# Taking whole-tile elementwise work off GpSimd in a statically scheduled four-layer graph network

## Chip, cores, metric

One NeuronCore of a Trainium2 chip. The metric is the device time of one execution in microseconds (us). Ratios are the mean time of one kernel's runs over the mean of the other kernel's runs of the same rounds, so they differ a little from the ratio of the medians that are quoted.

## What is computed

In this kernel TensorE (PE in the views) does the matrix products and leaves them in PSUM, a memory of banks; ScalarE (ACT) and VectorE (DVE) read them out, which is called an eviction below, and work elementwise; GpSimd (POOL) works elementwise too. GAT is a graph attention layer.

64 graphs of 256 nodes with 256 features pass four layers, each with a residual and a norm:

```python
x = _layernorm(x + L0(x, adj))   # 8-head masked attention, norm, feed-forward (256 -> 1024 -> 256), norm
x = _layernorm(x + L1(x, adj))   # GAT: softmax_m(leaky(f_n + g_m) masked) @ (x W^T) + bias
x = _layernorm(x + L2(x, adj))   # GAT, then elu
x = _layernorm(x + L3(x, adj))   # two relational graph convolutions with elu
```

L1 adds `attn1[:, :, None] + attn2[:, None, :]`, applies leaky_relu (slope 0.2), masks, and takes a softmax. All products are float32.

## The kernel before

The kernel doesn't issue instructions as it meets them. It records operations of all graphs (engine, assumed cost, tiles read and written), lets a list scheduler choose one static order, and then issues them in that order; every engine works through its own part of it in sequence.

```python
class Plan:
    LAG = {"PE": 0.21, "DVE": 0.13, "ACT": 0.13, "POOL": 0.08, "SP": 3.5}
    SWITCH = 0.3                       # assumed cost of a change of matmul shape on TensorE
    # op(): dependencies by tile, or by part of a tile: (t, part)
    # schedule(): earliest operation of the oldest graph that can start, engine by engine [cut]
...
        for o in plan.schedule():
            o.issue()
```

`port="uses"` marks operations of VectorE and GpSimd that the plan never lets overlap across these two engines. PSUM is held by a ring of four one-bank tiles ("bank") and a single four-bank tile ("wide"), which QKV, the scores and the feed-forward use in turn:

```python
                    act(1.02, ... nc.scalar.activation(ph(), s()[:, :, hg, :], AF.Exp, accum_out=...), [s], [ph])
                    # masks of p: first half on VectorE, second half on GpSimd
                    op("DVE" if hg == 0 else "POOL", 1.14 if hg == 0 else 2.1, mask, [ph, am], [ph], port="uses")
...
            def feed_forward(x1, xt):
                add_row(xt, ln2b)                                     # GpSimd
                ...                                                   # x1 *= ln1g, x1 += b2: GpSimd
                hid, w = new("hid", [P, NF, N]), new("wide", None)
                def chunk(f):
                    return w()[:, f % 4, f // 4, :]                   # bank f % 4
                for f in range(NF):                                   # 8 chunks
                    pe("full", 0.86, ... product(chunk(f), w1.., x1T..), [x1T], [(w, f % 4)], [hid])
                    act(0.36, ... activation(hid()[:, f, :], chunk(f), AF.Relu, bias=..), [(w, f % 4)], [(hid, f)])
                y = product_plus(... w2 ..., x1)
                mv, rstd = statistics(y, False)
                # apply: four fused VectorE steps: (y - mean) * ln2g, then * rstd + xt
                dve(2.4, apply, [y, mv, rstd, xt], [y], "uses")
                layer_norm(y)
```

A norm is bn_stats and bn_aggr on VectorE, four operations on 128x2 elements on GpSimd (rstd and the shift), and the application on ScalarE. The GAT's score chain:

```python
                for i in range(NB):
                    act(0.36, ... activation(e()[:, i, :], pf(), AF.Identity, bias=g_i), [pf, (h, i)], [(e, i)])
                dve(0.60, ... e = max(0.2 * e, e))
                act(0.52, ... e = exp(e))
                dve(0.60, ... e = min(e, gm))                         # gm is 1e30 on an edge, else 1e-30
```

## Time and profile before

| | before |
|---|---|
| time, median | 3626.88 us (3623.37 to 3631.0, 4 runs) |
| TensorE busy | 3220.8 us, 89% |
| VectorE, ScalarE, GpSimd busy | 2294.5, 1587.1, 1591.0 us |
| mean granted TensorE clock | 0.959 |
| TensorE waits, all rows of its view summed | 397.8 us |

In the profile, lines such as `PE wide L561 <- ACT hid L707` name who waited (TensorE, for an instruction writing tile wide), for whom (ScalarE's instruction writing hid), then total us, times and longest. The reading is in the prediction below.

### The profile page before, as it was taken

How to read it: one execution, taken by the hardware profiler on the slowest of the kernel's cores; microseconds unless marked ns; L12 is line 12 of the kernel's file. 1: busy time of each engine (PE TensorE's matmuls, PEld its weight loads, DVE VectorE, ACT ScalarE, POOL GpSimd, SP SyncE). 2: the span in 40 equal slices, each digit the busy share in tenths (PEclk: the TensorE clock that was granted, in tenths of full speed). 3: DMA queues.
4: the chain of work that ended last, by engine and by line, in shares of the span. 5: the costliest groups of instructions: out<-in, count | busy, mean ns of one | idle time of the engine just before them, and what ended most of it. 6: DMA issues, size and time to landing. Idle time of an engine off the chain costs nothing.

```text
span 3632.6 us, 50464 instructions
## 1 busy us (share of the span) xinstructions
PE 3220.8 (89%) x18742; PEld 2357.1 (65%) x18742; DVE 2294.5 (63%) x4960; ACT 1587.1 (44%) x3393; POOL 1591.0 (44%) x2325
## 2 busy tenths in 40 slices
PE   5899998998988998989998989998998998998985
PEld 4666766666666766666766666766666766666663
DVE  3457656666666666666666666666666666666653
ACT  1334544444444444444444444444444444444442
POOL 3334444445444444444444444444444444354441
PEclk9999999999999999999999999999999999999997
DMA  4000000000010000010000000000000000000000
GB/s 121 12 15 30 30 24 21 27 24 30 18 30 21 30 21 24 23 30 21 27 24 21 27 30 21 27 24 21 27 30 21 27 24 21 27 30 24 12 4 10
DMA packets 91947, 93.64 MB, mean 26 GB/s; under 512 B 5648, under 2 KB 90896, under 8 KB 91696
## 3 DMA queue, kind: packets, MB, share of 16 engines
q1 hardware_dynamic: 87040, 83.91, 7.5%
q10 hardware_dynamic: 4032, 5.24, 0.4%
q8 instruction: 151, 2.47, 0.3%
q0 software_dynamic: 624, 1.19, 0.2%
q14 instruction: 100, 0.82, 0.1%
HBM read 73.54 MB, written 16.78 MB: 25 GB/s over the span
## 4 chain that ended last, share of the span: by engine, by line
PE 73%; DVE 11%; ACT 9%; POOL 3%; issue 2%; DMA 0%; SPq 0%; POOLq 0%; DVEq 0%; ACTq 0%
PE bank L561 42%; PE wide L561 20%; PE bank L673 5%; PE bank L552 4%; ACT hid L707 3%; ACT X L589 2%; PE wide L650 2%; DVE st L570 2%; DVE e L747 2%; ACT p L656 2%; DVE o L829 1%; DVE mv L571 1%; DVE X L689 1%; POOL rstd L577 1%; POOL rstd L575 1%
## 5 line engine op out<-in xcount | busy, mean ns | idle before, releaser
L561 PE MATMUL wide<-T,W1T 128*128 128x256 f32 x2048 | 535.2, 396 | 124.9 <-ACT hid L707 86.3
L561 PEld LDWEIGHTS wide<-T,W1T 128*128 128x128 f32 x2048 | 371.0, 192 | 264.3 <-ACT hid L707 153.6
L561 PE MATMUL bank<-cw,T 128*128 128x512 f32 x1024 | 471.3, 603 | 3.1 <-ACT T L555 3.0
L561 PE MATMUL bank<-W2T,hid 128*128 128x256 f32 x2048 | 465.5, 381 | 0.2 <-DVE X L773 0.2
L561 PEld LDWEIGHTS bank<-W2T,hid 128*128 128x128 f32 x2048 | 385.1, 190 | 53.0 <-issue 1.8
L574 POOL TENSOR_SCALAR rstd<-mv 128x2 f32<-128x2 f32 x384 | 104.7, 273 | 673.1 <-DVE mv L571 659.7
L589 ACT ACTIVATE X<-X,rstd 128x256 f32<-128x256 f32 x512 | 279.1, 595 | 261.8 <-POOL rstd L578 261.4
L707 ACT ACTIVATE hid<-wide,col_b 128x256 f32<-128x256 f32 x512 | 229.3, 471 | 292.8 <-PE wide L561 292.6
L561 PE MATMUL bank<-h,e 128*128 128x259 f32 x1024 | 304.8, 444 | 40.4 <-DVE e L747 40.1
L660 POOL TENSOR_TENSOR p<-p,am 128x1024 f32<-128x1024 f32 x128 | 278.0, 2172 | 138.8 <-ACT p L656 138.8
L561 PEld LDWEIGHTS bank<-cw,T 128*128 128x128 f32 x1024 | 193.4, 192 | 208.7 <-issue 188.6
L656 ACT ACTIVATE p<-wide 128x1024 f32<-128x1024 f32 x256 | 259.9, 1019 | 154.4 <-PE wide L650 154.4
L575 POOL TENSOR_TENSOR rstd<-rstd,neghalf 128x2 f32<-128x2 f32 x384 | 290.8, 757 | 32.0
L561 PEld LDWEIGHTS bank<-h,e 128*128 128x128 f32 x1024 | 218.2, 221 | 99.9 <-DVE e L747 59.6
L677 DVE RECIPROCAL inv<-bank 128x256 f32<-128x256 f32 x128 | 223.7, 1748 | 67.7 <-PE bank L673 67.6
L570 DVE BATCH_NORM_STATS2 st<-X 128x6 f32<-128x256 f32 x640 | 259.1, 405 | 8.7 <-POOL X L777 5.0
L561 PE MATMUL wide<-T,WqkvT 128*128 128x256 f32 x1024 | 251.0, 393 | 10.5 <-ACT p L656 9.3
L561 PE MATMUL bank<-gw,T 128*128 128x258 f32 x1024 | 249.9, 386 | 4.0 <-ACT T L555 2.6
L650 PE MATMUL wide<-qk 32*128 32x256 f32 x2048 | 162.6, 435 | 98.6 <-ACT p L656 93.4
L555 ACT COPY T<-bank 128x512 f32<-128x512 f32 x384 | 217.9, 589 | 65.9 <-PE bank L552 65.5
L845 POOL TENSOR_TENSOR o<-o,X 128x512 f32<-128x512 f32 x64 | 91.9, 1436 | 332.1 <-DVE o L829 332.1
L660 DVE TENSOR_TENSOR p<-p,am 128x1024 f32<-128x1024 f32 x128 | 186.5, 1457 | 65.5 <-ACT p L656 65.1
(126 smaller groups left out, 5801.0 us busy)
## 6 DMA issues: line engine op xcount, KB each, us to landing
adj<-in_adj_dram SPq DMA_DIRECT2D x128, 256.0 KB, 3.5
x<-in_x_dram SPq DMA_DIRECT2D x64, 256.0 KB, 2.7
xr<-in_x_dram SPq DMA_DIRECT2D x64, 256.0 KB, 2.7
out_dram<-o SPq DMA_DIRECT2D x64, 256.0 KB, 2.2
W1T<-in_W1T_dram ACTq DMA_DIRECT2D x1, 1024.0 KB, 9.5
W2T<-in_W2T_dram ACTq DMA_DIRECT2D x1, 1024.0 KB, 16.1
WqkvT<-in_WqkvT_dram ACTq DMA_DIRECT2D x1, 768.0 KB, 4.8
cw<-in_w_root_dram ACTq DMA_DIRECT2D x2, 256.0 KB, 12.6
```

What stands on the lines that cost most here:

```text
L552: nc.tensor.transpose(pt()[:, kb, i * P : (i + 1) * P], xt()[:, i, kb * P : (kb + 1) * P], ident)
L555: act(0.48, lambda: nc.scalar.copy(xT(), pt()), [pt], [xT])
L561: nc.tensor.matmul(dst, lhsT=lhs(c), rhs=rhs(c), start=(c == 0), stop=(c == n - 1))
L570: nc.vector.bn_stats(stat()[:, i, :], y()[:, i, :])
L575: nc.gpsimd.tensor_tensor(rstd()[:, 0, :], rstd()[:, 0, :], neghalf[:, 0:NB], op=ALU.pow)
L589: nc.scalar.activation(y()[:, i, :], y()[:, i, :], AF.Identity, bias=rstd()[:, 1, i : i + 1], scale=rstd()[:, 0, i : i + 1])
L650: nc.tensor.matmul(s()[:, r, hg, :], lhsT=qk()[f, KB + hg, kt * P : (kt + 1) * P], rhs=qk()[f, hg, :], start=True, stop=True)
L656: act(1.02, lambda ph=ph, k=k, s=s, hg=hg: nc.scalar.activation(ph(), s()[:, :, hg, :], AF.Exp, accum_out=seen_sum[:, k : k + 1]), [s], [ph])
L660: eng.tensor_tensor(ph(), ph(), am()[:, kt, None, :].to_broadcast([P, 4, N]), op=ALU.mult)
L673: nc.tensor.matmul(pc()[32 * r : 32 * r + 32, dst, :], lhsT=lhsT, rhs=p[kt, hg]()[:, r, :], start=(kt == 0), stop=(kt == NB - 1))
L677: dve(1.67, lambda hg=hg, pc=pc: nc.vector.reciprocal(inv()[:, hg, :], pc()[:, 1, :]), [pc], [(inv, hg)])
L707: act(0.36, lambda f=f: nc.scalar.activation(hid()[:, f, :], chunk(f), AF.Relu, bias=b1[:, f : f + 1]), [(w, f % 4)], [(hid, f)])
```

## The change

Its intent is to leave GpSimd little but the norms' 128x2 operations, so that its long whole-tile operations neither stand in chains nor block VectorE. The core of the diff (a constant tile for the bias, the checks at the end, repeated edits and a new sequence of the norms' bn_stats and bn_aggr are cut):

```diff
-            def add_row(xt, row):
-                pool(1.23, lambda: nc.gpsimd.tensor_tensor(xt(), xt(), row[...], op=ALU.add), [xt], [xt])
+            def with_row(xt, row, op):
+                dve(0.60, lambda: nc.vector.tensor_tensor(xt(), xt(), row[...], op=op), [xt], [xt], "uses")
+            def add(xt, yt):
+                dve(0.60, lambda: nc.vector.tensor_tensor(xt(), xt(), yt(), op=ALU.add), [xt, yt], [xt], "uses")
...
-                dve(0.33, ... tensor_scalar(gm(), pt(), BIG, TINY, op0=ALU.mult, op1=ALU.max), [pt], [gm])
+                dve(0.33, ... tensor_scalar(gm(), pt(), BIG, NO_EDGE, op0=ALU.mult, op1=ALU.add), [pt], [gm])   # -346
...
-                        op("DVE" if hg == 0 else "POOL", 1.14 if hg == 0 else 2.1, mask, [ph, am], [ph], port="uses")
+                        dve(1.14, mask, [ph, am], [ph], "uses")
...
-                pool(1.23, lambda: nc.gpsimd.tensor_tensor(seen_inv, seen_inv, inv(), op=ALU.add), [inv], [])
+                act(0.61, lambda: nc.scalar.activation(inv(), inv(), AF.Identity, accum_out=seen_inv[:, g : g + 1]), ...)
...   (feed-forward)
-                dve(2.4, apply, [y, mv, rstd, xt], [y], "uses")        # four fused steps
+                layer_norm(y)                                          # applied on ScalarE
+                with_row(y, ln2g, ALU.mult)
+                add(y, xt)
                 layer_norm(y)
...   (GAT)
-                    act(0.29, ... copy(h()[:, i, 0 : D + 2], ph()), [ph], [(h, i)])
+                    # layer 1: the bias is added in the eviction, on VectorE (0.34); layer 2 as before
...
-                    act(0.36, ... activation(e()[:, i, :], pf(), AF.Identity, bias=g_i), ...)
+                    dve(0.40, ... scalar_tensor_tensor(e()[:, i, :], pf(), g_i, gm()[:, i, :], op0=ALU.add, op1=ALU.min), ...)
...
-                dve(0.60, lambda: nc.vector.tensor_tensor(e(), e(), gm(), op=ALU.min), [e, gm], [e], "uses")
...   (layer 2: elu and residual in three fused VectorE steps; the last residual by add)
```

More of the change, by code (lines that the diff above doesn't have):

```diff
@@ L21 @@
 BIG = 1e30
-TINY = 1e-30
+NO_EDGE = -346.0
 RINGS = {"x": 3, "adj": 4, "bits": 2, "am": 2, "gm": 6, "T": 5, "qk": 2, "v": 2, "p": 6, "inv": 1, "ctxT": 2, "X": 9,
@@ L266, in weight, with rows @@
         return w
-    def rows(name):
+    def rows(name, zeros=0):
         v = t[name]
         n = v.shape[0]
-        w = const.tile([P, n], F32, tag=f"row_{name}", name=f"row_{name}")
-        nc.gpsimd.dma_start(w, bass.AP(tensor=v.tensor, offset=v.offset, ap=[[0, P], [1, n]]))
+        w = const.tile([P, n + zeros], F32, tag=f"row_{name}", name=f"row_{name}")
+        if zeros:
+            nc.vector.memset(w[:, n:], 0.0)
+        nc.gpsimd.dma_start(w[:, 0:n], bass.AP(tensor=v.tensor, offset=v.offset, ap=[[0, P], [1, n]]))
         return w
@@ L331, in tile_gnn_stack @@
     seen_sum = filled([P, 4 * B], F32, "seen_sum", 0.0)
-    seen_inv = filled([P, KB, N], F32, "seen_inv", 0.0)
+    seen_inv = filled([P, B], F32, "seen_inv", 0.0)
     seen_fg = filled([P, 2 * B, NB, 2], F32, "seen_fg", 0.0)
@@ L354, in tile_gnn_stack @@
     gat1 = gat_weights(1, "L1_WT", "L1_W")
-    gbias = rows("L1_bias")
+    gbias = rows("L1_bias", 2)
     gat2 = gat_weights(2, "L2_W", "L2_WT")
@@ L539, in load @@
                 return xt
-            def add_row(xt, row):
-                pool(1.23, lambda: nc.gpsimd.tensor_tensor(xt(), xt(), row[:, None, :].to_broadcast([P, NB, D]),
-                                                           op=ALU.add), [xt], [xt])
+            def with_row(xt, row, op):
+                dve(0.60, lambda: nc.vector.tensor_tensor(xt(), xt(), row[:, None, :].to_broadcast([P, NB, D]), op=op),
+                    [xt], [xt], "uses")
+            def add(xt, yt):
+                dve(0.60, lambda: nc.vector.tensor_tensor(xt(), xt(), yt(), op=ALU.add), [xt, yt], [xt], "uses")
             def transposed(xt):
@@ L561, in product, with layer_norm @@
                     nc.tensor.matmul(dst, lhsT=lhs(c), rhs=rhs(c), start=(c == 0), stop=(c == n - 1))
-            def statistics(y, shift):
+            def layer_norm(y):
                 mv, stat = new("mv", [P, NB, 2]), new("st", [P, NB, 6])
@@ L570, in stats @@
                         nc.vector.bn_stats(stat()[:, i, :], y()[:, i, :])
+                    for i in range(NB):
                         nc.vector.bn_aggr(mv()[:, i, :], stat()[:, i, :])
                 def root():
-                    nc.gpsimd.tensor_scalar(rstd()[:, 0, :], mv()[:, :, 1], EPS, None, op0=ALU.add)
+                    nc.gpsimd.tensor_scalar(rstd()[:, 0, :], mv()[:, :, 1], 1.0, EPS, op0=ALU.mult, op1=ALU.add)
                     nc.gpsimd.tensor_tensor(rstd()[:, 0, :], rstd()[:, 0, :], neghalf[:, 0:NB], op=ALU.pow)
-                    if shift:
-                        nc.gpsimd.tensor_tensor(rstd()[:, 1, :], mv()[:, :, 0], rstd()[:, 0, :], op=ALU.mult)
-                        nc.gpsimd.tensor_scalar(rstd()[:, 1, :], rstd()[:, 1, :], -1.0, None, op0=ALU.mult)
-                dve(1.08, stats, [y], [mv, stat])
-                pool(1.56 if shift else 1.0, root, [mv], [rstd], port="waits")
-                return mv, rstd
-            def layer_norm(y):
-                mv, rstd = statistics(y, True)
+                    nc.gpsimd.tensor_tensor(rstd()[:, 1, :], mv()[:, :, 0], rstd()[:, 0, :], op=ALU.mult)
+                    nc.gpsimd.tensor_scalar(rstd()[:, 1, :], rstd()[:, 1, :], -1.0, 1.0, op0=ALU.mult, op1=ALU.mult)
                 def apply():
@@ L590, in apply @@
                                              scale=rstd()[:, 0, i : i + 1])
+                dve(1.0, stats, [y], [mv, stat])
+                pool(1.5, root, [mv], [rstd], port="waits")
                 act(1.0, apply, [y, rstd], [y])
@@ L606, in masks @@
                 pe("full", 0.22, issue, [bits], [pt], [am, gm])
-                dve(0.33, lambda: nc.vector.tensor_scalar(gm(), pt(), BIG, TINY, op0=ALU.mult, op1=ALU.max), [pt], [gm])
+                dve(0.33, lambda: nc.vector.tensor_scalar(gm(), pt(), BIG, NO_EDGE, op0=ALU.mult, op1=ALU.add), [pt], [gm])
                 dve(0.33, lambda: nc.vector.tensor_tensor(am(), pt(), bits(), op=ALU.max), [pt, bits], [am])
@@ L657, in attention, with mask @@
                             ph(), s()[:, :, hg, :], AF.Exp, accum_out=seen_sum[:, k : k + 1]), [s], [ph])
-                        def mask(ph=ph, kt=kt, eng=nc.vector if hg == 0 else nc.gpsimd):
-                            eng.tensor_tensor(ph(), ph(), am()[:, kt, None, :].to_broadcast([P, 4, N]), op=ALU.mult)
-                        op("DVE" if hg == 0 else "POOL", 1.14 if hg == 0 else 2.1, mask, [ph, am], [ph], port="uses")
+                        def mask(ph=ph, kt=kt):
+                            nc.vector.tensor_tensor(ph(), ph(), am()[:, kt, None, :].to_broadcast([P, 4, N]), op=ALU.mult)
+                        dve(1.14, mask, [ph, am], [ph], "uses")
                 inv = new("inv", [P, KB, N])
@@ L679, in attention @@
                         ctxT()[:, hg, :], pc()[:, 0, :], inv()[:, hg, :], op=ALU.mult), [pc, (inv, hg)], [(ctxT, hg)])
-                pool(1.23, lambda: nc.gpsimd.tensor_tensor(seen_inv, seen_inv, inv(), op=ALU.add), [inv], [])
+                act(0.61, lambda: nc.scalar.activation(inv(), inv(), AF.Identity, accum_out=seen_inv[:, g : g + 1]), [inv], [inv])
                 return ctxT
@@ L692, in feed_forward @@
             def feed_forward(x1, xt):
-                add_row(xt, ln2b)
+                with_row(xt, ln2b, ALU.add)
                 x1T = transposed(x1)
-                pool(1.23, lambda: nc.gpsimd.tensor_tensor(x1(), x1(), ln1g[:, None, :].to_broadcast([P, NB, D]),
-                                                           op=ALU.mult), [x1], [x1])
-                add_row(x1, b2)
+                with_row(x1, ln1g, ALU.mult)
+                with_row(x1, b2, ALU.add)
                 hid, w = new("hid", [P, NF, N]), new("wide", None)
@@ L709, in feed_forward, with gat @@
                 y = product_plus(lambda c: hid()[:, c, :], [hid], lambda c: w2[:, c, :], NF, x1)
-                mv, rstd = statistics(y, False)
-                def apply():
-                    for i in range(NB):
-                        yi = y()[:, i, :]
-                        nc.vector.scalar_tensor_tensor(yi, yi, mv()[:, i, 0:1], ln2g, op0=ALU.subtract, op1=ALU.mult)
-                        nc.vector.scalar_tensor_tensor(yi, yi, rstd()[:, 0, i : i + 1], xt()[:, i, :],
-                                                       op0=ALU.mult, op1=ALU.add)
-                dve(2.4, apply, [y, mv, rstd, xt], [y], "uses")
+                layer_norm(y)
+                with_row(y, ln2g, ALU.mult)
+                add(y, xt)
                 layer_norm(y)
                 return y
-            def gat(xt, w, gm, seen, finish):
+            def gat(xt, w, gm, seen, bias, finish):
                 xT = transposed(xt)
@@ L729, in gat @@
                                                                 lambda kb: w[:, kb, :], KB), [xT], [ph], [h])
-                    act(0.29, lambda i=i, ph=ph: nc.scalar.copy(h()[:, i, 0 : D + 2], ph()), [ph], [(h, i)])
+                    if bias is None:
+                        act(0.29, lambda i=i, ph=ph: nc.scalar.copy(h()[:, i, 0 : D + 2], ph()), [ph], [(h, i)])
+                    else:
+                        dve(0.34, lambda i=i, ph=ph: nc.vector.tensor_tensor(h()[:, i, 0 : D + 2], ph(), bias, op=ALU.add),
+                            [ph], [(h, i)])
                 pool(0.1, lambda: (nc.gpsimd.memset(h()[:, :, ONE : ONE + 1], 1.0)), [], [(h, "one")], None)
@@ L742, in gat @@
                 for i in range(NB):
-                    act(0.36, lambda i=i: nc.scalar.activation(e()[:, i, :], pf(), AF.Identity,
-                                                               bias=h()[:, i, G_COL : G_COL + 1]), [pf, (h, i)], [(e, i)])
-                dve(0.60, lambda: nc.vector.scalar_tensor_tensor(e(), e(), SLOPE, e(), op0=ALU.mult, op1=ALU.max), [e], [e], "uses")
+                    dve(0.40, lambda i=i: nc.vector.scalar_tensor_tensor(e()[:, i, :], pf(), h()[:, i, G_COL : G_COL + 1],
+                                                                         gm()[:, i, :], op0=ALU.add, op1=ALU.min),
+                        [pf, (h, i), gm], [(e, i)])
+                dve(0.60, lambda: nc.vector.scalar_tensor_tensor(e(), e(), SLOPE, e(), op0=ALU.mult, op1=ALU.max), [e], [e],
+                    "uses")
                 act(0.52, lambda: nc.scalar.activation(e(), e(), AF.Exp), [e], [e])
-                dve(0.60, lambda: nc.vector.tensor_tensor(e(), e(), gm(), op=ALU.min), [e, gm], [e], "uses")
                 for i in range(NB):
@@ L757, in finish @@
                 def finish(i, z, po, r):
-                    if i == 0:
-                        add_row(xt, gbias)
                     dve(0.40, lambda: nc.vector.scalar_tensor_tensor(z()[:, i, :], po()[:, 0:D], r(), xt()[:, i, :],
                                                                      op0=ALU.mult, op1=ALU.add), [po, r, xt], [(z, i)])
-                z = gat(xt, gat1, gm, 2 * g, finish)
+                z = gat(xt, gat1, gm, 2 * g, gbias, finish)
                 layer_norm(z)
@@ L768, in finish @@
                 def finish(i, z, po, r):
-                    n = new("n", [P, D])
+                    n, zi = new("n", [P, D]), lambda: z()[:, i, :]
                     act(0.36, lambda: nc.scalar.activation(n(), po()[:, 0:D], AF.Exp, scale=r()), [po, r], [n])
-                    dve(0.30, lambda: nc.vector.tensor_scalar(n(), n(), 1.0, -1.0, op0=ALU.min, op1=ALU.add), [n], [n], "uses")
-                    dve(0.40, lambda: nc.vector.scalar_tensor_tensor(z()[:, i, :], po()[:, 0:D], r(), n(), op0=ALU.mult,
-                                                                     op1=ALU.max), [po, r, n], [(z, i)])
-                z = gat(xt, gat2, gm, 2 * g + 1, finish)
-                pool(1.23, lambda: nc.gpsimd.tensor_tensor(z(), z(), xt(), op=ALU.add), [z, xt], [z])
+                    dve(0.40, lambda: nc.vector.scalar_tensor_tensor(zi(), po()[:, 0:D], r(), xt()[:, i, :], op0=ALU.mult,
+                                                                     op1=ALU.add), [po, r, xt], [(z, i)])
+                    dve(0.37, lambda: nc.vector.scalar_tensor_tensor(n(), n(), 1.0, xt()[:, i, :], op0=ALU.min,
+                                                                     op1=ALU.add), [n, xt], [n], "uses")
+                    dve(0.37, lambda: nc.vector.scalar_tensor_tensor(zi(), n(), -1.0, zi(), op0=ALU.add, op1=ALU.max),
+                        [n, (z, i)], [(z, i)], "uses")
+                z = gat(xt, gat2, gm, 2 * g + 1, None, finish)
                 layer_norm(z)
@@ L835, in graph @@
             xT = transposed(xt)
-            add_row(xt, bo)
+            with_row(xt, bo, ALU.add)
             ctxT = attention(xT, am)
@@ L844, in graph @@
             h = conv(conv(xt, conv_w[0], conv_b[0], rel, rdeg), conv_w[1], conv_b[1], rel, rdeg)
-            pool(1.23, lambda: nc.gpsimd.tensor_tensor(h(), h(), xt(), op=ALU.add), [h, xt], [h])
+            add(h, xt)
             layer_norm(h)
@@ L860, in tile_gnn_stack @@
     nc.vector.tensor_reduce(worst[:, 0:1], seen_sum, AX.X, ALU.max)
-    nc.vector.tensor_reduce(worst[:, 1:2], seen_inv.rearrange("p h n -> p (h n)"), AX.X, ALU.add)
+    nc.vector.tensor_reduce(worst[:, 1:2], seen_inv, AX.X, ALU.max)
     nc.vector.tensor_reduce(worst[:, 2:3], seen_fg.rearrange("p g n k -> p (g n k)"), AX.X, ALU.max)
@@ L973, in general_layer1 @@
         z = general_gat("x3", xt, gat1, mask, ALU.add)
-        add_row(z, gbias)
+        add_row(z, gbias[:, 0:D])
         nc.gpsimd.tensor_tensor(z, z, xt, op=ALU.add)
```

## The prediction

> **What bounds the kernel now.** I read the page's busy shares first, then the slices, the waits of TensorE, and the timeline around the longest wait. In the shares the columns are busy time, share of the span and instructions; in the slices each digit is a tenth.
>
> ```profile
> span 3632.6 us, 50464 instructions
> ## 1 busy us (share of the span) xinstructions
> PE 3220.8 (89%) x18742; PEld 2357.1 (65%) x18742; DVE 2294.5 (63%) x4960; ACT 1587.1 (44%) x3393; POOL 1591.0 (44%) x2325
> ...
> PEclk9999999999999999999999999999999999999997
> ```
>
> TensorE is the bound: 89% busy, the others far behind. Its idle time is about 412 us, and its mean granted clock, in the view of the cores, is 0.959: (1 - 0.959) x 3632.6 = 149 us more, if work at the lower clock is taken to last longer in proportion. The change takes no matmul away, so only these two sums can shrink. Who keeps TensorE waiting (total us, times, longest):
>
> ```profile
> PE wide L650 <- ACT p L656: 93.4, 29, 3.6
> PE wide L561 <- ACT hid L707: 86.3, 162, 1.2
> PE bank L552 <- ACT X L589: 48.7, 67, 6.5
> PE wide L561 <- ACT p L656: 47.7, 34, 2.6
> PE bank L561 <- DVE e L747: 40.1, 30, 5.7
> ```
>
> Attention's exp frees the only four-bank PSUM tile ("wide") for 93.4 + 47.7 = 141 us of waits; the feed-forward evictions make 86, the norms' last step 49, the GAT softmax 40. No row names GpSimd: it acts only through ScalarE and VectorE. From about 850 us the work repeats, two graphs in 109.25 us (54.6 per graph; 64 of these are 3494 us, so head and tail add about 138). In one repeat, with PE, ACT, DVE and POOL rows picked out:
>
> ```profile
> 1489.73 1.02 ACT L656 ACTIVATE p<-wide 128x1024 f32<-128x1024 f32 x1 [0.73 <-PE wide L650]
> ...
> 1490.74 0.83 ACT L743 ACTIVATE e<-bank,h 128x256 f32<-128x256 f32 x2
> ...
> 1491.45 1.09 ACT L589 ACTIVATE X<-X,rstd 128x256 f32<-128x256 f32 x2
> ...
> 1492.44 1.02 ACT L656 ACTIVATE p<-wide 128x1024 f32<-128x1024 f32 x1
> ...
> 1493.60 1.78 PE L650 MATMUL wide<-qk 32*128 32x256 f32 x16 [3.58 <-ACT p L656]
> 1493.63 2.13 POOL L660 TENSOR_TENSOR p<-p,am 128x1024 f32<-128x1024 f32 x1 [2.92 <-ACT p L656]
> 1494.10 2.20 DVE L747 TENSOR_TENSOR e<-e,gm 128x512 f32<-128x512 f32 x1 [1.40 <-ACT e L746]
> ...
> 1496.35 3.82 PE L561 MATMUL bank<-h,e 128*128 128x259 f32 x8 [0.97 <-DVE e L747]
> ```
>
> Between the two exps of one score tile ScalarE does GAT work (e) and a norm (X), so the next scores wait 3.58 us. Then VectorE's mask of the GAT takes 2.20 us beside GpSimd's mask of p, and TensorE waits 0.97 more. After that TensorE is slow: the same 8 h,e matmuls take 1.91 us elsewhere in the repeat. The view by windows gives the granted clock there:
>
> ```profile
> 1490.00:1493.50 3.50, 0.02 (x1) 0.00 (x0) 1.83 (x2) 3.50 (x9) 0.59 (x3) 1.00 0.00 0
> 1493.50:1500.40 6.90, 5.82 (x28) 3.71 (x32) 3.78 (x5) 3.16 (x7) 4.38 (x3) 0.53 0.00 0
> ```
>
> Columns: window, length, busy time of PE, weight loads, DVE, ACT, POOL, then clock. After 3.5 us without a matmul, 6.9 us go at about half clock, once in every repeat.
>
> **What the Trainium skill says.** "TensorE: Matmul & The Clock Gate", part 1, on what is actually happening: the array falls to half rate after about one idle window of 3.4 us and returns after one busy window. The two windows above agree: a 3.58 us wait, then 0.53. "SBUF — State Buffer", who interferes with whom: a VectorE instruction with two SBUF inputs contends with a GpSimd instruction that reads SBUF, and the second to start is blocked until the first ends. This agrees: the 2.20 us e,gm is 0.69 us elsewhere in the timeline, and p on VectorE has a mean of 1457 ns but 1.19 us at 1442.72. "GPSIMD Engine Reference", key points: elementwise work is structurally about 2x faster on VectorE; here p's mask is 2172 against 1.19 us, a row addition 1.27 to 1.44 against 0.69 for a 128x512 VectorE operation.
>
> **The change, part by part** (busy us over the run).
> - GpSimd loses p's mask 278, four row additions and one row product (90 + 83 + 86 + 82 + 82), two residuals (83 + 92) and the sum of inv (83): 959. The feed-forward's first norm gains two operations, 64 x (0.30 + 0.25) = 35. 1591 falls to about 670, all small and mostly off the shared reads.
> - VectorE gains p's mask, 128 x 1.19 = 152; seven whole-tile operations a graph (bo, ln2b, ln1g, b2, ln2g, two residuals), 448 x 0.69 = 309; the GAT's limit straight from PSUM, 256 x 0.48 = 123; layer 1's bias in the eviction, 128 x 0.42 = 54; layer 2's third fused step, about 184 - 106 = 78. It loses the GAT minimum 129 and the feed-forward's two fused steps 222, and, with GpSimd out of the way, about 70 of stretching (p 33, the leaky step 18, conv's last step 18). Sum 2294 + 716 - 421 = about 2590, of a span near 3460: 75%. Beside TensorE, not the bound.
> - ScalarE loses the GAT additions 107 and half of the h copies 48, gains the norm's apply 128 x 0.55 = 70 and inv's sum with its accumulator read, about 50: 1587 to about 1552. Little in sum, but what leaves sat between two exps.
> - The GAT chain from spread to product was ScalarE twice, VectorE leaky, ScalarE exp, VectorE minimum; it loses the last, at least 0.69 us and one hand-over. The feed-forward's norm grows longer by the ScalarE hop.
> - **The order.** The static order is chosen by a scheduler from assumed costs, so moving work reshuffles all engines. I compared both TensorE orders: same products, other interleaving. I summed the TensorE work standing between one score block and the next user of "wide" (durations from the dense stretches of the trace before: 0.44 us a product of 256 columns, 0.86 of 512, 0.9 us for 8 value products). Exp needs about 2.75 us (two at 1.0 + 0.1 and the hand-overs). Where less work stands between, the rest is a wait. Before: 68.0 + 11.9 + 52.7 = 133 us for next scores, next QKV, next feed-forward; the trace has 141, so the count is sound. After: 9.6 + 41.6 + 7.3 = 58. Gain about 75 to 80 us. Scores followed by scores, whose 3.58 us wait stops the clock, mostly find 2.2 to 13.5 us of other work now; QKV straight after scores, about 2.7 us, comes once in seven graphs.
>
> **The sum.** Exp waits: -78. Clock: 25 repeats x 6.8 us x half = 85 us of the 149 belong to that one wait; I take 55 to 60 back, since new gaps may reach 3.4 us. GAT: 40 to about 25, -15. Feed-forward evictions: 86, left. Norms and evictions behind a fuller VectorE: +25 new waits (a guess). Head and tail: about -25 to -35, as a single graph's chain there is bare and its GpSimd steps of 1.3 us become 0.7. Total about -155: 3625 - 155 = 3470; I say 3465.
>
> **The rivals.**
> 1. VectorE becomes the bound in stretches. For: 63% rises to 75%, eviction and p mask share one in-order queue, and the assumed costs (0.33 for an eviction) are below the measured 0.42. TensorE would wait for DVE rows now small (DVE qk 15.0, DVE ctxT 4.3). Against: a quarter stays free. It would bring the time to 3540 to 3620.
> 2. GpSimd's work was hidden anyway, so only the order changes. For: no TensorE row names GpSimd. Against: the e,gm row shows it acting through the shared reads. With the clock dips kept, only the exp waits go: about 3540 to 3560.
> 3. The dips go entirely and feed-forward waits shrink with ScalarE's freer queue: 3370 to 3400.
> 4. The norm's small operations, on GpSimd still, are blocked by VectorE's more numerous two-input operations, and the wait on X (49) doubles: +50.
>
> **Range and chances.** TensorE's own work is 109.25 - 10.1 (waits) - 3.4 (clock) = 95.7 us a repeat, 47.9 a graph; with 138 of ends 3200 us is the floor of this design. Of the present 6.7 us of loss a graph I expect about 4.3 to stay. From 3.0 to 5.7, the range is 3385 to 3560. Two per cent faster is under 3552: 0.88. Same 0.10, slower 0.02.
>
> **What would show it.** TensorE's waits on exp near 60 us, none of 3.58 repeating; mean clock 0.97 or above; busy DVE near 2590, POOL near 670, ACT near 1550; the p mask near 1200 ns for all 256; a longer repeat of seven graphs at some 51.5 to 52.5 us each. I am wrong if TensorE waits for DVE over 120 us in all (rival 1), or the clock stays at 0.96 (rival 2), or the rstd operations exceed 1.58 us together by half (rival 4).

## The result

The changed kernel took 3574.91 us (median of 4, 3567.63 to 3583.18) against 3626.88: ratio 0.9857, 95% interval 0.983 to 0.9884. It is about 52 us faster, under two per cent, where 3465 us, and at most 3560, had been expected. The head of its page:

```profile
span 3576.9 us, 50759 instructions
## 1 busy us (share of the span) xinstructions
PE 3204.5 (90%) x18742; PEld 2345.8 (66%) x18742; DVE 2451.6 (69%) x5665; ACT 1550.4 (43%) x3265; POOL 742.0 (21%) x1813
...
PEclk8999999999999999999999999999999999999997
```

The engines' loads moved about as worked out (ScalarE 1550 where 1552 was said, GpSimd 742 for 670, VectorE 2452 for 2590). The mean clock is 0.970. TensorE's waits in the changed kernel, with the same columns as before; L566 is before's L561, L706 its L707, L587 its L589:

```profile
PE wide L566 <- ACT hid L706: 126.4, 205, 1.2
PE wide L566 <- ACT p L656: 27.9, 19, 2.2
PE bank L673 <- DVE p L660: 22.2, 10, 2.4
PE wide L650 <- ACT v L631: 20.0, 17, 1.7
PE bank L566 <- ACT T L560: 19.4, 42, 2.0
PE wide L650 <- ACT hid L706: 16.3, 10, 1.9
PE bank L557 <- ACT X L587: 16.1, 33, 6.0
PE bank L557 <- DVE rdeg L794: 12.7, 7, 1.8
PE bank L566 <- ACT e L744: 11.1, 13, 4.6
```

Exp (p) went from 141.1 to 30.6 us, the norms' step (X) from 48.7 to 16.1, the GAT softmax (e) from 40.3 to 11.1. The three rows aimed at gave 172 us. But hid rose from 89.7 to 142.7, and all other rows rose together from 78.0 to 156.7, most of it in rows that had been small (p on VectorE, v, T, rdeg, rel). Of 172 us, 132 came back; the waits fell by 40.6 in all, from 397.8 to 357.2. With 16.3 us less of TensorE's busy time this makes up the 55.7 us by which the two profiled executions differ.

In the steady part the work repeats every seven graphs, in about 378.9 us: 54.1 us a graph, where before had 54.6 and 51.5 to 52.5 had been expected. So of the 56 us, about 32 come from 64 graphs of the steady part and about 24 from head and tail. Here is the feed-forward in one of these repeats, TensorE and ScalarE rows of the timeline picked out (start, length, engine, line, operation, tiles; in brackets the idle time before it and what ended it):

```profile
1839.54 1.99 PE L566 MATMUL wide<-T,W1T 128*128 128x256 f32 x8 [0.62 <-ACT hid L706]
1841.57 0.84 ACT L706 ACTIVATE hid<-wide,col_b 128x256 f32<-128x256 f32 x2 [1.11 <-PE wide L566]
1842.46 1.13 PE L566 MATMUL wide<-T,W1T 128*128 128x256 f32 x4 [0.93 <-ACT hid L706]
1843.63 0.47 ACT L706 ACTIVATE hid<-wide,col_b 128x256 f32<-128x256 f32 x1 [1.22 <-PE wide L566]
1844.15 1.13 PE L566 MATMUL wide<-T,W1T 128*128 128x256 f32 x4 [0.56 <-ACT hid L706]
1845.32 0.47 ACT L706 ACTIVATE hid<-wide,col_b 128x256 f32<-128x256 f32 x1 [1.22 <-PE wide L566]
1845.85 1.13 PE L566 MATMUL wide<-T,W1T 128*128 128x256 f32 x4 [0.56 <-ACT hid L706]
```

A chunk, its eviction, the next chunk, its eviction: strictly in turn, although the chunks lie in four different banks. ScalarE isn't late; it is idle for 1.22 us before each eviction. The built program explains it: in its semaphore waits (a semaphore is a counter by which one engine waits for another), each access of "wide" waits for the last opposite access of the whole tile that was issued before it. Chunk 5 waits for the eviction of chunk 3, which itself was issued after chunk 4 and so waits for chunk 4. The kernel's own scheduler keeps dependencies by bank (`(w, f % 4)`) and plans these to overlap. This is the first theory.

**Theory A**: the chain of matmul and eviction through the four-bank tile, which the scheduler doesn't know of, took back what the exp waits gave. **Theory B**: VectorE is too full and what it evicts comes late. **Theory C**: the change's time isn't a property of the moved work at all, but of the order that the scheduler happened to find. **Theory D**: GpSimd's long operations were what cost, wherever they stand in the order.

### The profile page after: what moved, and what is told of

It is laid out like the page before. It is cut to its first block, busy times and chain, and to the rows that moved or that the text cites. A ratio compares the mean times of both kernels' runs of the same rounds, so it can differ in the third digit from the quotient of the medians.

```text
span 3576.9 us, 50759 instructions
## 1 busy us (share of the span) xinstructions
PE 3204.5 (90%) x18742; PEld 2345.8 (66%) x18742; DVE 2451.6 (69%) x5665; ACT 1550.4 (43%) x3265; POOL 742.0 (21%) x1813
## 3 DMA queue, kind: packets, MB, share of 16 engines
q0 software_dynamic: 624, 1.19, 0.2%
## 4 chain that ended last, share of the span: by engine, by line
PE 66%; DVE 19%; ACT 9%; issue 3%; POOL 2%; DMA 0%; SPq 0%; ACTq 0%; POOLq 0%
PE bank L566 37%; PE wide L566 20%; PE bank L673 4%; ACT hid L706 4%; PE bank L557 3%; DVE p L660 2%; ACT X L587 2%; PE wide L650 2%; DVE inv L677 2%; DVE st L575 2%; ACT p L656 1%; DVE X L768 1%; DVE X L544 1%; DVE mv L577 1%; DVE o L821 1%
## 5 line engine op out<-in xcount | busy, mean ns | idle before, releaser
L566 PE MATMUL wide<-T,W1T 128*128 128x256 f32 x2048 | 535.9, 396 | 132.3 <-ACT hid L706 126.4
L566 PEld LDWEIGHTS wide<-T,W1T 128*128 128x128 f32 x2048 | 371.2, 192 | 256.3 <-ACT hid L706 205.0
L580 POOL TENSOR_SCALAR rstd<-mv 128x2 f32<-128x2 f32 x384 | 126.0, 328 | 1775.4 <-DVE mv L577 1599.4
L566 PE MATMUL bank<-cw,T 128*128 128x512 f32 x1024 | 475.4, 607 | 12.8 <-ACT T L560 12.3
L566 PE MATMUL bank<-W2T,hid 128*128 128x256 f32 x2048 | 474.3, 386 | 0.0
L587 ACT ACTIVATE X<-X,rstd 128x256 f32<-128x256 f32 x640 | 347.8, 593 | 279.0 <-POOL rstd L583 242.2
L566 PEld LDWEIGHTS bank<-W2T,hid 128*128 128x128 f32 x2048 | 391.6, 194 | 64.9 <-issue 12.8
L706 ACT ACTIVATE hid<-wide,col_b 128x256 f32<-128x256 f32 x512 | 229.1, 471 | 403.0 <-PE wide L566 402.0
L660 DVE TENSOR_TENSOR p<-p,am 128x1024 f32<-128x1024 f32 x256 | 308.0, 1216 | 94.2 <-ACT p L656 93.3
L566 PEld LDWEIGHTS bank<-cw,T 128*128 128x128 f32 x1024 | 192.7, 194 | 221.2 <-issue 188.5
L581 POOL TENSOR_TENSOR rstd<-rstd,neghalf 128x2 f32<-128x2 f32 x384 | 316.6, 824 | 32.0
L566 PE MATMUL wide<-T,WqkvT 128*128 128x256 f32 x1024 | 256.7, 394 | 28.9 <-ACT p L656 24.2
L566 PE MATMUL bank<-h,e 128*128 128x259 f32 x1024 | 264.0, 399 | 20.4 <-ACT e L744 11.1
L566 PE MATMUL bank<-gw,T 128*128 128x258 f32 x1024 | 254.2, 386 | 4.7 <-ACT T L560 3.8
L566 PEld LDWEIGHTS bank<-h,e 128*128 128x128 f32 x1024 | 198.1, 198 | 75.7 <-issue 31.5
L575 DVE BATCH_NORM_STATS2 st<-X 128x6 f32<-128x256 f32 x640 | 239.4, 416 | 5.4
L566 PEld LDWEIGHTS wide<-T,WqkvT 128*128 128x128 f32 x1024 | 191.0, 194 | 76.0 <-ACT p L656 29.3
L566 PEld LDWEIGHTS bank<-gw,T 128*128 128x128 f32 x1024 | 189.5, 191 | 58.2 <-issue 18.8
L810 ACT CAST hi<-bank 128x256 fp32r<-128x256 f32 x256 | 93.8, 370 | 296.1 <-DVE o L813 265.5
```

Of the source, the lines that this page charges most:

```text
L566: nc.tensor.matmul(dst, lhsT=lhs(c), rhs=rhs(c), start=(c == 0), stop=(c == n - 1))
L575: nc.vector.bn_stats(stat()[:, i, :], y()[:, i, :])
L580: nc.gpsimd.tensor_scalar(rstd()[:, 0, :], mv()[:, :, 1], 1.0, EPS, op0=ALU.mult, op1=ALU.add)
L581: nc.gpsimd.tensor_tensor(rstd()[:, 0, :], rstd()[:, 0, :], neghalf[:, 0:NB], op=ALU.pow)
L587: nc.scalar.activation(y()[:, i, :], y()[:, i, :], AF.Identity, bias=rstd()[:, 1, i : i + 1], scale=rstd()[:, 0, i : i + 1])
L660: nc.vector.tensor_tensor(ph(), ph(), am()[:, kt, None, :].to_broadcast([P, 4, N]), op=ALU.mult)
```

## The experiments

Each kernel was correct. The columns hid, exp and X of the tables are sums of the rows of TensorE's waits on ACT hid, ACT p and ACT X.

### Feed-forward chunks in one-bank tiles, in both kernels (theories A, B)

```diff
-                hid, w = new("hid", [P, NF, N]), new("wide", None)
+                hid = new("hid", [P, NF, N])
+                ws = [new("bank", [P, 2, N]) for _ in range(NF // 2)]
                 def chunk(f):
-                    return w()[:, f % 4, f // 4, :]
+                    return ws[f // 2]()[:, f % 2, :]
                 for f in range(NF):
+                    w = ws[f // 2]
-                    ... [x1T], [(w, f % 4)], [hid])      # and the eviction's [(w, f % 4)]
+                    ... [x1T], [(w, f % 2)], [hid])      # likewise (w, f % 2)
```

> The kernel after, with the feed-forward's eight chunks in four one-bank PSUM tiles of the ring that all other products use, in place of the one four-bank tile. In the program as built, the scheduler's issue order makes each chunk of the four-bank tile wait for the eviction of the chunk before, in a chain of matmul, eviction, matmul. Theory A (this chain took the gain): waits of TensorE on hid fall from 142 us (126 + 16) to under 40, and the time from 3575 to 3450-3510. Theory B (VectorE is fuller and everything it evicts comes late): hid waits fall but waits on DVE and on free banks take their place, 3560-3600. A sub-rival: the four banks are short, waits on T, e and DVE rows rise, 3580 or more.

> The kernel before with the feed-forward's chunks in one-bank tiles, as in the run that does so to the kernel after. Theory A: hid waits 90 fall to under 30, and, with the four-bank tile free of the feed-forward, exp waits fall too; 3520-3560. If the two changes are independent, after with banks lies below this by the same 51 us. If this lies as low as after with banks, the change's worth was only in the reshuffling.

The kernel after with this: 3491.72 us, ratio to before 0.9624, as theory A has it. The kernel before with this: **3402.33 us**, ratio 0.9377 (0.9362 to 0.9393), which beats both kernels and lies 118 us below what theory A had expected. In after with one-bank tiles the chunks now run through, and evictions lie beside them:

```profile
1850.73 3.62 PE L566 MATMUL bank<-T,W1T 128*128 128x256 f32 x16
1852.66 0.47 ACT L708 ACTIVATE hid<-bank,col_b 128x256 f32<-128x256 f32 x1 [0.47 <-PE bank L566]
1854.02 1.21 ACT L708 ACTIVATE hid<-bank,col_b 128x256 f32<-128x256 f32 x3
```

Four chunks take 3.62 us without a break. Waits on hid fell from 142.7 to 6.5 us in the one pair and from 89.7 to 8.8 in the other. TensorE's busy time on the chunks fell too, from 535.9 to 483.4 us and from 535.2 to 488.6: a chunk between two breaks takes 1.13 us, and here four take 3.62. The chain is shown as a loss. Two things remain open. The edit also leaves the only four-bank tile to QKV and the scores, and in before the exp waits fell with it, from 141.1 to 40.4 us; no run splits the tile and keeps that sharing, so what follows is the worth of both together. And theory A in its simple form is not the whole answer: with the chain gone, the changed kernel is 89 us *slower* than the unchanged one.

### Parts of the change (theories B, D)

> The kernel after with one half of the masks of p back on GpSimd (128 of 2.1 us). VectorE loses about 155 us of busy time, GpSimd gains 278. Theory B (VectorE's load holds the gain back): faster than after, 3530-3560, and the waits on DVE p (22), rel (11), rdeg (16) shrink. Theory A (the chain of evictions): the hid waits stay at 110-150 and the time within 20 us of 3575. Rival C (GpSimd's large operations slow VectorE through the shared reads): 3590-3620.

The edit puts back `op("DVE" if hg == 0 else "POOL", ...)` in after. 3568.16 us, ratio 0.9829 (0.9812 to 0.9846), against 0.9857 (0.983 to 0.9884) for after: the intervals overlap, no difference shown. VectorE's masks fell by 148 us, but it lost only 63 us of busy time, as other VectorE instructions took longer again (the addition of row_b 918 ns, not 691). Theory B's waits did shrink: the rows on VectorE fell from 78.6 to 32.6 us in all, p from 22.2 to none, rel from 10.9 to 4.4, rdeg from 16.0 to 0.9. But exp rose from 30.6 to 76.7, and the time did not follow; B's 3530 to 3560 isn't there. The plan changed as well here, so this is another order.

> The kernel before with only the GAT scores' part of the change: limit from PSUM on VectorE ahead of exp, nothing on ScalarE between spread and exp, no minimum after it. If the gain of the change is the GAT's (what stood between attention's two exps): the exp waits fall from 141 to under 70, waits on e from 40 to under 15, time 3570-3595. If the gain comes from GpSimd's large operations leaving: within 15 us of 3626.

The edit is the GAT hunk of the diff alone, applied to before. 3640.76 us, ratio 1.0047 (1.0026 to 1.0067): a little slower. The exp waits did fall, from 141.1 to 81.3 us, and those on e from 40.3 to 26.1, neither as far as expected, and hid rose from 89.7 to 129.0. One wait was exchanged for the other, as in the full change.

### The order nudged, the work unchanged (theory C)

```diff
-    SWITCH = 0.3
+    SWITCH = 0.2      # second pair: 0.4
```

> The kernel before with one constant of the scheduler nudged (the assumed cost of TensorE's change between matmul shapes 0.3 to 0.2): the same work in another order. If the change's 51 us is a property of the moved work, this stays within 15 us of 3626. If the time hangs on which order the scheduler happens to find, it moves by 20 to 80 us either way; its hid waits, from the count of back-to-back chunks, go up to 110-130, which says 3640-3680.

> The kernel after with the same nudge. Property of the work: within 15 us of 3575, and still some 50 below its partner. Accident of the order: off by 20 us or more, the difference to its partner changed by as much as the effect itself. The count of back-to-back chunks is a little above that of after: hid waits 125-150.

> The kernel before with the same constant nudged the other way (0.3 to 0.4). If orders scatter: somewhere in 3580-3670. The count of back-to-back chunks, higher than in any other, speaks for hid waits of 130-150.

> The kernel after, nudged to 0.4. If the change has a worth of its own under the scatter, the three pairs (0.2, 0.3, 0.4) average to after being faster; so far the differences are -51 and +78. Scatter alone: 3560-3670, no sign kept.

| four-bank tile | before: us | hid, exp, X | after: us | hid, exp, X |
|---|---|---|---|---|
| 0.2 | 3589.63 | 131, 66, 23 | 3667.17 | 134, 72, 48 |
| 0.3 | 3626.88 | 90, 141, 49 | 3574.91 | 143, 31, 16 |
| 0.4 | 3637.56 | 147, 53, 26 | 3620.03 | 134, 65, 20 |
| mean | 3618.0 | | 3620.7 | |

The counts of back-to-back chunks told the hid waits (none is over 1 us outside the range expected), but not the times: before at 0.2 was expected at 3640 to 3680 and took 3589.63.

This is the central result. One constant, which changes no instruction but their order, moves before by up to 48 us and after by up to 92. The differences between the two kernels are +78, -52 and -18. Their mean is +3 us. The 52 us is one draw. And the case's before is the odd one of its three orders: few hid waits and many exp waits, where the others, like all of after, have it the other way round.

The same with one-bank tiles:

> The kernel before with one-bank tiles for the feed-forward, same nudge. It was 3402. Property: 3390-3415. Accident of the order: 3420-3480, near the kernel after with banks.

> The kernel after with one-bank tiles, same nudge. It was 3492. If moving the work costs 90 us once the chain of evictions is gone: 3475-3510, still far above its partner. Accident of the order: the difference between the two shrinks below 45 or turns round.

> The kernel before with one-bank feed-forward tiles, constant nudged to 0.4: the third order. Scatter: 3400-3470. Whatever the order, hid waits under 15 us and below every order with the four-bank tile (3575).

> The kernel after with one-bank tiles, nudged to 0.4. If the change has a worth of its own here: below its partner by over 40. If it costs: above by over 40. If only orders differ: within 40 of its partner, 3420-3490.

| one-bank tiles | before: us | X | after: us | X |
|---|---|---|---|---|
| 0.2 | 3439.41 | 37 | 3440.49 | 46 |
| 0.3 | 3402.33 | 38 | 3491.72 | 62 |
| 0.4 | 3416.30 | 40 | 3449.47 | 53 |
| mean | 3419.3 | | 3460.6 | |

Each kernel against its own four-bank partner, the split is worth 150, 225 and 221 us in before (0.2, 0.3, 0.4) and 227, 83 and 171 in after: 179 in the mean, and every one of the six one-bank kernels is faster than every four-bank one. The change itself is slower by 1, 89 and 33 here.

### The order held, the work moved (theories C, D)

In the next kernel the scheduler still plans GpSimd's large operations (ten a graph in the built program, not nine as the expectation says) as GpSimd's, but they are issued on VectorE. The orders of TensorE and ScalarE are the same, instruction by instruction.

```diff
-                pool(1.23, lambda: nc.gpsimd.tensor_tensor(...         # all five kinds
+                pool(1.23, lambda: nc.vector.tensor_tensor(...
-                        def mask(ph=ph, kt=kt, eng=nc.vector if hg == 0 else nc.gpsimd):
+                        def mask(ph=ph, kt=kt, eng=nc.vector):
```

> The kernel before with all nine of GpSimd's large operations a graph issued on VectorE instead, while the scheduler plans as if GpSimd did them: the orders of TensorE and ScalarE are word for word those of before. If the moved work itself carries the gain (shorter on VectorE, no stretching), 3540-3600. If the gain was only the new order: 3610-3650, with exp waits still near 141 and the 3.58 us wait and its half-clock stretch still in every repeat. If VectorE's load is the trouble: above 3660, waits on DVE rows up by 60 or more.

3710.16 us, ratio 1.0229 (1.0206 to 1.0252): 84 us slower. Its waits of TensorE:

```profile
PE wide L650 <- ACT p L656: 93.3, 29, 3.6
PE wide L561 <- ACT hid L707: 85.3, 162, 0.7
PE bank L552 <- ACT X L589: 67.8, 108, 5.9
PE wide L561 <- ACT p L656: 47.6, 34, 2.6
PE wide L561 <- DVE qk L629: 45.0, 27, 2.8
```

The exp and hid rows are before's to within a microsecond: they belong to the order, not to where the elementwise work runs. What the move brought is longer waits on X (48.7 to 67.8), on VectorE's qk (15.0 to 45.0) and on ScalarE's hi (1.4 to 26.2), while those on e fell (40.1 to 16.5). All rows on VectorE together rose only from 75.2 to 87.2, not by the 60 expected of too full a VectorE. The likely reason, argued and not shown, is that these operations now stand in VectorE's queue at places chosen for another engine: after's VectorE is nearly as busy (2451.6 us, here 2514.8) and has X at 16.1 and qk at 9.2.

> The reverse: the kernel after, its TensorE order unchanged, with half of p's masks, the row operations and the two residual additions issued on GpSimd at the places where VectorE did them (the bias in the eviction, the GAT limit and inv's sum stay). Each takes 1.3 or 2.1 us in place of 0.69 or 1.2 and blocks VectorE. If where the work runs matters: 3620-3700. If only the order matters: within 20 us of 3575.

The reverse, after's order with half the masks, the rows and two residuals issued on GpSimd: 3623.23 us, ratio to before 0.9998; that is 0.9998 / 0.9857 = 1.014 of after, across two sets of runs. So placement does count when the order is held, in whichever direction the order wasn't planned for. Theory D, which has GpSimd's work cost in any order, fails on the first of these two runs.

### A scheduler that knows the whole-tile waits

```diff
-                t, part = a if isinstance(a, tuple) else (a, None)
+                t, part = (a[0] if isinstance(a, tuple) else a), None
```

> The kernel before, its scheduler told that every access waits for the whole tile (parts of a tile no longer count as independent), as the built program's waits have it. Theory A': the scheduler then fills the waits that it can see, 3560-3610, below the mean of its three blind orders (3618). If the blind spot is not the trouble: within the scatter, 3590-3640. The count of back-to-back chunks (155 us) says hid waits stay large: it had nothing to put between.

> The kernel after with the same knowledge in its scheduler. Its count of back-to-back chunks is 105 us against 155 of its partner. Theory A' with a worth of the change (the shorter chains now pay): 3500-3560 and at least 40 below its partner. If the change is worth nothing: within 25 of its partner.

A miss: 3741.91 and 3693.80 us, slower than all blind orders. In h_before hid took 186 us and the mean clock fell to 0.946. Knowing of the chain did not help. The edit makes every tile whole in the plan, not wide alone, so which of the lost overlaps cost is not shown; splitting the tile is what helped. With one-bank tiles this rule couldn't be built for before: the scheduler found no order ("the rings are too small"). The pair differs by -48 us, which one pair cannot tell from scatter.

### Undoing the feed-forward norm's part, with one-bank tiles

In all three one-bank pairs after waits longer on X. The part that lengthens a norm's chain is the feed-forward's first norm. These runs undo it alone:

```diff
-                layer_norm(y)
-                with_row(y, ln2g, ALU.mult)
-                add(y, xt)
+                mv, rstd = statistics(y)
+                dve(1.6, fused, [y, mv, rstd, xt], [y], "uses")   # before's four fused steps
                 layer_norm(y)
```

> After with one-bank tiles, the feed-forward's first norm applied as before by four fused VectorE steps, without the ScalarE hop (planned at 1.6 us). If this part is what costs: waits on X fall from 62 to about 40 and the time from 3492 to 3430 or less. If not: X above 50, time within 3440-3500.

> The same in the second order (constant 0.2), partner 3440 with X 46. If this part costs: X below 42, time 3400-3430. If it is scatter: 3430-3480.

3421.95 and 3404.87 us, against 3491.72 and 3440.49: 70 and 36 us faster. X fell from 62.3 to 45.0 and from 45.9 to 23.9. The rows that answer, first from after with one-bank tiles:

```profile
PE bank L557 <- ACT X L587: 62.3, 76, 7.0
```

and with the norm undone, the same wait in the first order:

```profile
PE bank L557 <- ACT X L594: 45.0, 69, 7.2
```

The mean of the two, 3413, is within 8 us of before with one-bank tiles in the same two orders (3421). So this part may be what makes the change slower with one-bank tiles, but that is not shown. The edit changes the planned costs too, so these are new orders: in the built programs TensorE's sequence differs from that of after with one-bank tiles at most places. Gains of 70 and 36 us stand against a scatter of 37 and 51 us among the one-bank orders of before and after. That 17 and 22 us less on X don't add up to 70 and 36 shows the same: other waits moved as well; in the second order, waits of wide on T are 125 us, and it is still the faster one. In favour of the part, both runs are faster than all three orders of after with one-bank tiles, and X fell in both, as expected.

## Why the prediction was wrong

- **"What bounds the kernel"** held. TensorE stayed at 90%, no other engine came near, and the floor was not touched.
- **"The change part by part"**: the loads of ScalarE and GpSimd came out near the working, and the masks ran at 1216 ns where 1.19 us was said. VectorE's was 139 us too high. Of this, 49 us is bn_stats and bn_aggr, which I had left unchanged: in their new sequence neighbours overlap in the trace (451.4 to 402.2 us over all, although one bn_stats took 416 ns, not 405); the rest is spread over many groups. None of it moved the end.
- **"The order"**: the count of TensorE work between scores and the next user of wide said 58 us of exp waits; measured 30.6. The direction was right and the fall larger than counted, 110 us for 75 to 80; but the count looked at this row alone.
- **Clock**: 55 to 60 us expected back. By the same estimate, (1 - 0.970) x 3576.9 = 107 us are left of 149, 42 us back; the other executions had 0.969 to 0.974. The dip that it named did go: the h,e products and the scores, which stood in it, took 50 us less of TensorE's busy time (304.8 + 162.6 to 264.0 + 153.4). But all products together took 16.3 us less only, so 34 came back in others. What failed is the assumption that the clock drops only after gaps of 3.4 us: the 3.58 us wait is gone, no wait of the steady part exceeds 2.42 us, and still half-clock stretches recur (last section).
- **Head and tail**: -25 to -35 expected; 3576.9 - 64 x 378.9 / 7 = 113, against 3632.6 - 64 x 109.25 / 2 = 137, so -24. About right.
- **"Feed-forward evictions: 86, left"** is the step that failed first. They became 142.7 with the rows before scores. I had read 86 us as a fixed tax of the work; it is a property of how tightly an order packs the eight chunks, and the order that separates scores packs chunks.
- **"Norms and evictions behind a fuller VectorE: +25 new waits (a guess)"** is the second. The rows outside exp, X, e and hid rose by 79 us. That VectorE's load is the reason is not shown: taking half the masks away again shortened its rows and changed no time.
- **The sum** is what failed as a whole. Of the 155 us, 57 came, 40.6 of waits and 16.3 of busy time. It took one row's gain from a new order and left the other rows of the old order standing. All rows of an order change together. The interval of 175 us was put round that sum, and no part of it came from asking how much the same work scatters under other orders. Three orders of each kernel would have said: 48 and 92 us, with no mean difference.
- **Rival 2** ("GpSimd's work was hidden anyway, so only the order changes") is the nearest to what the runs show, although its own figures, 3540 to 3560 with the clock dips kept, were not met either. **Rival 1** is not supported as a bound: TensorE's waits on VectorE are 78.6 us against 75.2 before, under its own mark of 120. **Rival 4**: the four rstd operations take 328 + 824 + 288 + 322 = 1762 ns against 1579, 12% more, and X went down, not up.

Open: why the many small rows rise in after's orders; how the split's worth divides between the broken chain and the freed four-bank tile; what the feed-forward norm's part is worth with the four-bank tile, where it wasn't undone; and whether a larger sample of orders would show a small worth of the change below some 40 us.

## What to carry to other kernels

When a scheduler or a tuned order decides who waits, a wait's total in the trace is a property of that order: before crediting or blaming a change, nudge something that changes the order alone, and take only effects larger than that scatter. Where a producer and a consumer alternate strictly although their banks differ and both have time, look in the built program for a dependency kept by whole tile, and split the tile: here that, with the four-bank tile freed for its other users, was worth 83 to 227 us in all six comparisons, where the moved work was worth nothing that three orders could show.

## What the Trainium skill lacked or had wrong

- "TensorE: Matmul & The Clock Gate", part 1, on what is actually happening, speaks of about one idle window of 3.4 us before the clock halves. In after's steady repeat the longest single wait of TensorE is 2.42 us, and half-clock stretches still follow. Below, a window of 3.41 us in which TensorE was busy for 1.27 us, and whose wait of 2.24 us is its longest, is followed by one at half clock (columns as in the prediction). In this trace the clock changes only on a grid of 3.41 us. Of the grid's windows at full clock from 150 to 3400 us, the 32 that half clock followed had TensorE busy for 29 to 57%, and those that full clock followed for 47% or more: a window about half empty was enough. The page's section on a second HAM failure mode does tell of frequent short idles that do this, without a length.

```profile
1883.92:1887.33 3.41, 1.27 (x18) 0.72 (x16) 3.34 (x10) 2.07 (x4) 0.90 (x3) 1.00 0.01 2
1887.33:1890.74 3.41, 3.31 (x8) 2.65 (x9) 2.78 (x3) 1.77 (x4) 1.53 (x3) 0.50 0.02 5
1890.74:1894.15 3.41, 3.41 (x50) 2.13 (x52) 2.97 (x8) 0.00 (x0) 0.00 (x0) 0.99 0.00 0
```

- No page has it that accesses to different banks of one PSUM tile can be put in sequence by the program's own semaphores: 142.7 us of waits on hid with one four-bank tile, 6.5 us with one-bank tiles.
- "GPSIMD Engine Reference", key points, that elementwise work is structurally about 2x faster on VectorE, was right for the operation (2172 against 1216 ns for a mask) and says nothing of the kernel: with TensorE's and ScalarE's orders held, moving it made the kernel 84 us slower.
